# Turning the normalized tokens of a token-shift layer: TensorE transposes against DMA moves and 32x32 block transposes on VectorE

## The chip, the cores and the metric

The kernel runs on one core of one Trainium2 chip. The metric is the device time of one execution in microseconds. The core has five engines that run side by side, each with its own queue of instructions in a fixed order: TensorE (PE, its weight loads are shown as PEld), VectorE (DVE), ScalarE (ACT), GpSimd (POOL) and SyncE (SP), which here issues the DMAs. Engines wait for each other through semaphores.

## The reference

All inputs are float32. A residual stream `x` of 8 batches x 512 tokens x 512 channels goes through four blocks, each on the layer norm of the stream and scaled by the tanh of a gate: a cross attention, a routed feed-forward, a second (masked, biased) cross attention, and a token-shift feed-forward, which is the block the change is in:

```python
def _layernorm(x, axis=-1, eps=1e-05): ...      # no scale, no shift

def _L1_ffn_ref(x, W_r, W_k, W_v, mu_r, mu_k):
    x_prev = concatenate([zeros((B, 1, C)), x[:, :-1, :]], axis=1)
    xr = mu_r * x + (1.0 - mu_r) * x_prev
    xk = mu_k * x + (1.0 - mu_k) * x_prev
    r = sigmoid(einsum('btc,dc->btd', xr, W_r))
    k = einsum('btc,dc->btd', xk, W_k)
    k_act = square(relu(k))
    return r * einsum('btc,dc->btd', k_act, W_v)

x = x + tanh(g_xattn[0]) * _L0_xattn_ref(_layernorm(x), ctx_1024, ...)
x = x + tanh(g_ffn[0])   * _L0_ffn_ref(_layernorm(x), ...)
x = x + tanh(g_xattn[1]) * _L1_xattn_ref(_layernorm(x), ctx_1024, mask, ...)
x = x + tanh(g_ffn[1])   * _L1_ffn_ref(_layernorm(x), W_r, W_k, W_v, mu_r, mu_k)
```

Per batch the token-shift block is three products of 512x512 by 512x512. `mu_r` and `mu_k` are vectors over the channels.

## The kernel before, in words

The whole residual `x` stays on the chip as 32 tiles of 128 tokens x 512 channels (tokens on the partitions), four tiles a batch. The matmuls contract over the partitions, so the normalized tokens must be turned: channels on the partitions, tokens along the row. `ChannelMix` does the token-shift block. Its parts:

- `start` loads mu and the weights `wk` and `wr` on SP's queue. It runs early in the second attention, long before the block. A weight tile has 128 partitions x 4 groups x 512; channel `128 j + p` is partition p of group j.
- `normalize(t)` is one ACT instruction: `(x - mean) * rstd` of tile t, into `xn` (batch 0) or into half of a pair `xn2` (the other batches). The pairs take the buffers `v0` and `v1`, one each.
- `transpose(t)` turns a tile: four PE transposes of 128x128 against the identity into a PSUM bank (L1515) and one ACT copy of 128x512 (L1516) into `yT`, which holds the batch as 128 channels x 4 groups x (1 + 512) tokens, with a zero column in front as the previous token of the first.
- `mix_chunk(b, m, c)` forms `xk` (m = 1) or `xr` (m = 0) for a group of channels: ACT scales the shifted tokens by `1 - mu` (L1529), DVE adds the tokens times `mu` (L1532).
- `sum_steps`, `left_steps` and `right_steps` (L91, L110) form the sums of quarters that the products need, on DVE in this stage (tiles `xks`, `xrs`, and `wvs` for the sums of the squared keys).
- `SevenProducts` multiplies two 512x512 matrices with seven products of 256x256 instead of eight (a Strassen-Winograd scheme). A piece is four matmul calls of the program, eight PE instructions, into one PSUM bank. `next()` emits one piece with its evacuation. The order is 1, 2, 6, 5, 7, 4, 3: p1 and p5 are copied out by ACT (L177, L192), the others are added by DVE (L183 p2, L188 p6, L198 p7, L212 p4, L217 p3). After p7, POOL adds the copy of p5 to two quarters (L203, L204), and p4 and p3 need these sums. When a quarter is complete, `finish` applies what follows: Relu and Square on ACT for the keys (L1583, L1584), the sigmoid on ACT for the gates (L1594), and for the values DVE's multiplication by gate and `r` (L1607), POOL's addition to `x` (L1610) and the output DMA (L1619; for the last batch DVE does the addition and the DMA is L1615, and the order is 1, 6, 5, 7, 4, 3, 2).
- PSUM banks come in rotation from two pools, two of three from `p_mm` (4 buffers) and one of three from `p_s` (2 buffers), six in all; `bank()` gives the next, to pieces and to transposes.

The order of the work of every compute engine is written out by hand: `run` walks over the batches, and for batch b emits the products keys(b), gates(b), values(b). Between the seven pieces of a product it emits a list of other steps, one list a piece ("turns"). All engines' instructions come out in that order, each on its own queue:

- keys(b): `xr` of batch b (four `mix_chunk`) and its sums, and in the first batches one DVE statistics step (bn_stats, L52) for a later tile;
- gates(b): the four transposes of batch b + 1 after pieces 2, 3, 4 and 5, the four `wvs` sums after pieces 3 to 6, `xk` of batch b + 1 after pieces 6 and 7;
- values(b): the sums of `xk` of batch b + 1, then the four `normalize` of batch b + 2, and in the first batches one statistics step.

Batch 0 is normalized and turned earlier, among the last slots of the attention (`in_slot`, stage "route"); batch 1 is normalized in its "end" stage. SP's queue isn't in the hand-written order in this last part: its DMAs stand as the scheduler of the framework put them. DMAs of this program share eight completion semaphores in turn, so each may also wait for the one eight before it.

Of the kernel before, what the change touches and what calls it, by code (L numbers as in the profile page):

```python
# [9 lines left out]
FP = mybir.dt.float32  # L10
I32 = mybir.dt.int32
BF = mybir.dt.bfloat16
AF = mybir.ActivationFunctionType
# [4 lines left out]
P = 128  # L18
B, S, D = 8, 512, 512
# [3 lines left out]
TB = S // P  # L23
NC = D // P
# [196 lines left out]
class CrossAttention:  # L221
# [338 lines left out]
    def normalize(self, t):  # L560

        nc, cm = self.nc, self.cm
        xn = self.norm.tile([P, D], FP, name="xn")
        nc.scalar.activation(
            xn, cm.x[:, t, :], AF.Identity, bias=cm.nmr[:, t, :], scale=cm.rstd[:, t, :]
        )
        self.biasless.append(t)
        if not self.opening:
            self.add_bias(2)
        self.xn[t] = xn  # L570
# [422 lines left out]
class RoutedFfn:  # L993
# [20 lines left out]
    def start(self):  # L1014

        nc, tc, es, (wc_in, bc_in, tie_in) = self.nc, self.tc, self.es, self.ins[:3]
        keep = es.enter_context(
            tc.tile_pool(name="mo_keep", bufs=1, side="right", reuse_waits="tile")
        )
        self.permT = keep.tile([NE, NG, G], FP, name="permT")  # L1020
        self.bc = keep.tile([NE, 1], FP, name="bc")
        self.tie = keep.tile([NE, 1, G], FP, name="tie")
        self.keep = keep
        self.wc = keep.tile([P, NC, NE], FP, name="wc", tag="wc")
        self.route = es.enter_context(
            tc.tile_pool(name="mo_route", bufs=2, side="right", reuse_waits="tile")
        )
        dram = es.enter_context(
            tc.tile_pool(name="mo_x", bufs=1, space=bass.MemoryType.DRAM)
        )  # L1030
        self.aside = dram.tile([B * S, D], FP, name="aside")
        nc.sync.dma_start(out=self.wc, in_=wc_in.rearrange("(c p) e -> p c e", p=P))
        nc.sync.dma_start(out=self.bc, in_=bc_in)
        nc.sync.dma_start(out=self.tie, in_=tie_in.partition_broadcast(NE))
# [340 lines left out]
class ChannelMix:  # L1375
# [16 lines left out]
    def start(self):  # L1392
        nc = self.nc
        wr_in, wk_in, wv_in, mu_in = self.ins
        self.pool = pool = self.es.enter_context(
            self.tc.tile_pool(name="cm_w", bufs=1, side="right", reuse_waits="tile")
        )
        self.mu = pool.tile([P, 2, NC], FP, name="mu")
        nc.sync.dma_start(out=self.mu, in_=mu_in)
        self.om = pool.tile([P, 2, NC], FP, name="om")  # L1400
        self.wk = self.load(pool.tile([P, NC, D], FP, name="wk"), wk_in)
        self.wr = self.load(pool.tile([P, NC, D], FP, name="wr"), wr_in)

    def load(self, w, w_in):
        self.nc.sync.dma_start(out=w, in_=w_in.rearrange("(c p) f -> p c f", p=P))
# [86 lines left out]

    def normalize(self, t, xn=None):
        nc, cm = self.nc, self.cm
        if xn is None:
            i = t % TB
            if i % 2 == 0:
                self.two = self.at.pool.tile([P, 2, D], FP, name="xn2", tag=f"v{i // 2}")
            xn = self.two[:, i % 2, :]
        self.xn[t] = xn  # L1500
        nc.scalar.activation(
            xn, cm.x[:, t, :], AF.Identity, bias=cm.nmr[:, t, :], scale=cm.rstd[:, t, :]
        )

    def transpose(self, t):

        nc = self.nc
        b, i = divmod(t, TB)
        if i == 0:
            self.yT[b] = self.at.work.tile([P, NC, S + 1], FP, name="yT", tag="xnT")  # L1510
            nc.gpsimd.memset(self.yT[b][:, :, 0:1], 0.0)
        xn = self.xn.pop(t)
        ps = self.bank((NC, P))
        for c in range(NC):
            nc.tensor.transpose(ps[:, c, :], xn[:, c * P : (c + 1) * P], self.cm.ident)  # L1515
        nc.scalar.copy(self.yT[b][:, :, i * P + 1 : (i + 1) * P + 1], ps)  # L1516
# [309 lines left out]
```

## Time and profile before

| what | value |
|---|---|
| median of 3 runs | 1355.15 us (1353.41 to 1357.96) |
| profiled execution | 1363.44 us, span 1361.6 us |
| clock granted to TensorE | 0.991 of full speed over the span |
| ACT copies of the turned tiles (L1516) | 32 x 0.589 us |
| PE transposes of the tiles (L1515) | 128, first at 964.1 us, last at 1301.6 us |
| normalizations (L1501) | 32, median 0.81 us |
| DMAs on SP from 1062 us on | 18 outputs, median 2.8 us (512 KB) and 2.2 us (256 KB) to landing |

The page shows per engine its busy time, share of the span and number of instructions. Below that come the span in 40 equal slices, with the busy share of each in tenths (9 is 90% or more). The chain that ended last is followed back from the last instruction, at each step to what released it or to the instruction ahead of it on its engine. Groups of instructions are listed as line, engine, operation, output<-input, shape and count, then busy us and mean ns of one, then the idle time before them and what ended it. A busy PE is not PE at its peak, since the ends of matmuls are modelled. The view by stretches gives for each stretch its length, then for PE, PEld, DVE, ACT and POOL the busy us with the number of instructions, then the granted clock, the share of DMA and GB/s. In a timeline a line is start, length, engine, line and what it does, and in square brackets how long the engine was idle before and what ended that.

### The profile page before, as it was taken

What the parts mean: (1) busy time and instruction counts of PE and PEld (TensorE: products, weight loads), DVE (VectorE), ACT (ScalarE), POOL (GpSimd) and SP (SyncE); (2) the same over time, 40 slices, a digit from 0 to 9 for tenths busy, and PEclk for the clock granted to TensorE, in tenths of its full rate; (3) what the DMA queues carried; (4) which work ended last, traced back from release to release, by engine and by line L of the source; (5) the groups of instructions that cost most, each with busy time, mean ns of one, the idle gap of its engine ahead of it and who ended that gap; (6) DMA issues with size and microseconds to landing.
All of it is one profiled execution on the core that took longest, in us unless ns stands there. A gap on an engine that the chain in (4) does not pass through costs nothing. (4 is left out here: it accounts for less than half of the span.)

```text
span 1361.6 us, 32823 instructions
## 1 busy us (share of the span) xinstructions
PE 1300.3 (95%) x13184; PEld 1031.4 (76%) x13184; DVE 1001.3 (74%) x1448; ACT 808.0 (59%) x2538; POOL 702.0 (52%) x624
## 2 busy tenths in 40 slices
PE   6998899999999988999999999999999999999997
PEld 6886677777776877888888666676766888888886
DVE  4876667777786676777788777777775787887776
ACT  1365878888774435444225778888875454554442
POOL 4854555655643001555797777777665234443331
PEclk9999999999999999999999989999999999999999
DMA  9501566666612356431401067667610000000000
GB/s 295 200 1 40 192 203 226 210 209 202 207 55 64 110 160 218 125 115 63 153 1 63 29 193 225 213 215 224 215 44 1 1 32 31 32 32 32 31 32 32
DMA packets 116237, 160.84 MB, mean 118 GB/s; under 512 B 6973, under 2 KB 71997, under 8 KB 116085
## 3 DMA queue, kind: packets, MB, share of 16 engines
q1 hardware_dynamic: 115797, 158.74, 36.0%
q8 instruction: 104, 1.70, 0.5%
q14 instruction: 48, 0.39, 0.1%
q10 hardware_dynamic: 288, 0.00, 0.0%
HBM read 93.84 MB, written 64.88 MB: 117 GB/s over the span
## 5 line engine op out<-in xcount | busy, mean ns | idle before, releaser
L721 ACT ACTIVATE pr<-s,nmx 128x120 f32<-128x120 f32 x768 | 273.0, 496 | 41.8 <-DVE nmx L710 26.3
L878 PE MATMUL ops<-wo,aT 128*128 128x512 f32 x512 | 240.3, 611 | 5.7 <-DVE prT L842 2.8
L731 POOL TENSOR_TENSOR pr<-pr,rs 128x960 f32<-128x960 f32 x88 | 160.0, 1820 | 141.6 <-DVE rs L727 139.8
L721 ACT ACTIVATION_READ_ACCUMULATOR pr<-s,nmx 128x1 f32 x768 | 194.1, 253 | 0.0
L878 PEld LDWEIGHTS ops<-wo,aT 128*128 128x128 f32 x512 | 93.3, 192 | 104.2 <-issue 91.1
L1349 POOL TENSOR_TENSOR r<-r,b 128x1024 f32<-128x1024 f32 x31 | 73.5, 2377 | 148.5 <-ACT r L1348 148.5
L710 DVE TENSOR_REDUCE nmx<-s 128x8 f32<-128x960 f32 x96 | 106.6, 1153 | 55.1 <-PE s L666 55.0
L793 DVE STREAM_TRANSPOSE pr<-pr 128x1024 f32<-128x1024 f32 x88 | 109.1, 1240 | 33.1 <-POOL pr L731 33.1
L165 PE MATMUL qps<-xnT,wq 128*128 128x256 f32 x512 | 119.0, 380 | 0.0
L165 PEld LDWEIGHTS qps<-xnT,wq 128*128 128x128 f32 x512 | 96.3, 189 | 23.3 <-issue 10.0
L52 DVE BATCH_NORM_STATS2 bnst<-x 128x6 f32<-128x512 f32 x128 | 87.5, 684 | 0.3
L759 POOL TENSOR_TENSOR pr<-pr,rs 128x960 f32<-128x960 f32 x32 | 58.1, 1822 | 41.0 <-DVE rs L758 30.7
L861 PE MATMUL aps<-prT,v 120*32 120x128 f32 x2048 | 70.1, 278 | 9.1 <-DMA prT<-plane 4.1
L1610 POOL TENSOR_TENSOR x<-x,cv 128x512 f32<-128x512 f32 x28 | 41.4, 1480 | 70.8 <-DVE cv L1607 70.8
L888 DVE SCALAR_TENSOR_TENSOR x<-ops,gates,x 128x512 f32<-128x512 f32 x64 | 47.9, 748 | 38.8 <-PE ops L878 38.3
L666 PE MATMUL s<-kT,qT 32*128 32x120 f32 x2048 | 73.9, 280 | 0.3 <-ACT pr L721 0.3
L666 PEld LDWEIGHTS s<-kT,qT 32*128 32x128 f32 x2048 | 67.4, 190 | 7.2 <-issue 5.3
L861 PEld LDWEIGHTS aps<-prT,v 120*32 120x32 f32 x2048 | 52.7, 110 | 22.7 <-issue 11.2
L1348 ACT COPY r<-rps 128x1024 f32<-128x1024 f32 x31 | 31.4, 1013 | 59.1 <-PE rps L1336 59.1
L1583 ACT ACTIVATE kT<-kT 128x512 f32<-128x512 f32 x32 | 20.1, 627 | 73.5 <-DVE kT L183 38.4
L1336 PE MATMUL rps<-ident,rT 128*128 128x128 f32 x512 | 61.9, 275 | 1.8 <-DVE rT L1316 1.4
L769 ACT ACTIVATE pr<-s,nmx 128x120 f32<-128x120 f32 x128 | 44.2, 371 | 29.0 <-DVE nmx L766 29.0
(239 smaller groups left out, 3139.9 us busy)
## 6 DMA issues: line engine op xcount, KB each, us to landing
plane<-pr SPq DMA_DIRECT2D x88, 512.0 KB, 3.5
prT<-plane SPq DMA_DIRECT2D x176, 240.0 KB, 4.0
w<-in_w_dram SPq DMA_DIRECT2D x32, 512.0 KB, 4.6
x<-in_x_dram SPq DMA_DIRECT2D x8, 1024.0 KB, 16.9
aside<-x SPq DMA_DIRECT2D x32, 256.0 KB, 3.1
x<-aside SPq DMA_DIRECT2D x8, 1024.0 KB, 10.2
out_dram<-x SPq DMA_DIRECT2D x14, 512.0 KB, 2.8
wk<-in_wk_dram SPq DMA_DIRECT2D x3, 1024.0 KB, 8.6
```

The source lines that it names most:

```text
L52: cm.nc.vector.bn_stats(st, cm.x[:, t, :])
L165: self.nc.tensor.matmul(ps[:, m, :], rows[:, k, m * n : (m + 1) * n], columns[:, k, :], start=(k == 0), stop=(k == 1),)
L666: nc.tensor.matmul(s[j // 2][:, j % 2, hc * LK : (hc + 1) * LK], self.qT[b][r : r + 32, hc, toks], self.kT[r : r + 32, hc, keys], start=no ...
L710: nc.vector.tensor_reduce(nmx[u], sv[u], AX.X, ALU.max, negate=True)
L721: nc.scalar.activation(dst, src, AF.Exp, bias=nmx[u][:, j, hc, :], accum_out=sm[:, u, j, hc : hc + 1],)
L731: nc.gpsimd.tensor_tensor(half[u], half[u], by, ALU.mult)
L759: nc.gpsimd.tensor_tensor(pr[:, js, :, :], pr[:, js, :, :], rs[:, js, :, :].to_broadcast([P, 2, NC, LK]), ALU.mult,)
L793: nc.vector.transpose(pr, pr)
L861: nc.tensor.matmul(out, self.v[b // 2][:LK, b % 2, h * HD : (h + 1) * HD], p, start=True, stop=True,)
L878: nc.tensor.matmul(ops, self.aT[t][:, c, :], self.wo[:, c, :], start=(c == 0), stop=(c == NC - 1),)
L1336: nc.tensor.transpose(ps[:, k // 4, (k % 4) * P : (k % 4 + 1) * P], self.rT[:, 16 * tq + 8 * h + k, :], self.cm.ident,)
L1349: nc.gpsimd.tensor_tensor(r, r, b2, ALU.add)
```

## The change

Tiles of batches 1 to 7 are no longer turned by PE. A transposition of 128x128 is split into two steps: a move that brings blocks of 32 tokens to the right quarter of the partitions, and a transposition within 32x32 blocks.

- `normalize` is as before, but after each second tile `move_rows` follows: SP writes the pair (256 tokens x 512 channels) to a DRAM tile `rows` and reads it back with four DMAs, one for each quarter q of 32 partitions, into a new tile of the same buffer. Partition `32 q + e` then holds, for the eight groups of 32 tokens, token e of the group and the 128 channels `128 q` to `128 q + 127` (512 bytes each).
- `transpose` for b > 0 is one DVE instruction of 128x512 (sixteen 32x32 blocks for each quarter) that writes straight into `yT`. The PSUM bank, the four PE transposes and the ACT copy are gone. It stands at the same places in the program's order.
- Channels lie differently now: group j of partition `32 q + e` is channel `128 q + 32 j + e`. So `wk` and `wr` are loaded with four DMAs each (`load_rows`), mu with eight, and batch 0, which PE still turns, is written by `normalize` in an order of channels that gives the same places.

In the built program PE has 112 transposes fewer, ACT 28 copies fewer and DVE 28 transposes more; the order of the others on PE, DVE, ACT and POOL is unchanged. In the gates DVE's order becomes L183, transpose, L188, wvs, transpose, wvs, transpose, L198, wvs, transpose, L212. On SP, from the second moved batch on, the order is: write of the first pair, write of the second, four reads of the first, two output DMAs, four reads of the second.

```diff
@@ class ChannelMix, start
-        nc.sync.dma_start(out=self.mu, in_=mu_in)
+        for m in range(2):
+            by_row = mu_in[:, m, :].rearrange("(j e) q -> q e j", j=NC)
+            for q in range(4):
+                nc.sync.dma_start(out=self.mu[32 * q : 32 * q + 32, m, :], in_=by_row[q])
         self.om = pool.tile([P, 2, NC], FP, name="om")
-        self.wk = self.load(pool.tile([P, NC, D], FP, name="wk"), wk_in)
-        self.wr = self.load(pool.tile([P, NC, D], FP, name="wr"), wr_in)
+        self.wk = self.load_rows(pool.tile([P, NC, D], FP, name="wk"), wk_in)
+        self.wr = self.load_rows(pool.tile([P, NC, D], FP, name="wr"), wr_in)
+
+    def load_rows(self, w, w_in):
+        rows = w_in.rearrange("(q j e) f -> q e j f", q=4, j=NC)
+        for q in range(4):
+            self.nc.sync.dma_start(out=w[32 * q : 32 * q + 32], in_=rows[q])
+        return w
@@ normalize
-        if xn is None:
-            i = t % TB
+        moved = xn is None
+        i = t % TB
+        if moved:
             if i % 2 == 0:
                 self.two = self.at.pool.tile([P, 2, D], FP, name="xn2", tag=f"v{i // 2}")
             xn = self.two[:, i % 2, :]
         self.xn[t] = xn
+        to, x = xn, cm.x[:, t, :]
+        if not moved:
+            to = xn.rearrange("p (j q e) -> p q j e", q=4, j=NC)
+            x = x.rearrange("p (q j e) -> p q j e", q=4, j=NC)
         nc.scalar.activation(
-            xn, cm.x[:, t, :], AF.Identity, bias=cm.nmr[:, t, :], scale=cm.rstd[:, t, :]
+            to, x, AF.Identity, bias=cm.nmr[:, t, :], scale=cm.rstd[:, t, :]
         )
+        if moved and i % 2:
+            self.move_rows(t - 1)
+
+    def move_rows(self, t):
+        nc = self.nc
+        plane = self.at.dram.tile([2 * P, D], FP, name="rows")
+        nc.sync.dma_start(out=plane.rearrange("(i p) d -> p i d", p=P), in_=self.two)
+        two = self.at.pool.tile([P, 2, D], FP, name="xn2", tag=f"v{t % TB // 2}")
+        quarters = plane.rearrange("(i e) (q d) -> q e i d", e=32, q=4)
+        for q in range(4):
+            nc.sync.dma_start(
+                out=two[32 * q : 32 * q + 32].rearrange("p i (q d) -> p (i q) d", q=4),
+                in_=quarters[q],
+            )
+        for n in range(2):
+            self.xn[t + n] = two[:, n, :]
@@ transpose
         xn = self.xn.pop(t)
+        if b > 0:
+            to = self.yT[b][:, :, i * P + 1 : (i + 1) * P + 1]
+            nc.vector.transpose(
+                to.rearrange("p j (q t) -> p q j t", q=4),
+                xn.rearrange("p (q j e) -> p q j e", q=4, j=NC),
+            )
+            return
         ps = self.bank((NC, P))
```

## The prediction

> **What bounds the kernel now.** I read the page first, then the chain that ended last, then one batch of the last stage engine by engine, then the waits. The page's engine line and its slices of TensorE say that PE is full almost everywhere, the last stage included:
>
> ```profile
> PE 1300.3 (95%) x13184; PEld 1031.4 (76%) x13184; DVE 1001.3 (74%) x1448; ACT 808.0 (59%) x2538; POOL 702.0 (52%) x624
> PE   6998899999999988999999999999999999999997
> ```
>
> The change works in the token-shift layer, from about 1040 us on. There a batch is three products of seven pieces (keys, gates, values), and the four transposes of the next batch stand among the pieces of the gates. I cut the stage at each start of the DVE instruction of L198 in the gates (piece p7); the view by stretches gives (span, then busy us of PE, PEld, DVE, ACT, POOL):
>
> ```profile
> 1185.36:1224.11 38.75, 38.57 (x186) 33.46 (x185) 31.46 (x44) 20.15 (x36) 16.04 (x15) 1.00 0.07 28
> 1224.11:1262.87 38.76, 38.57 (x186) 33.45 (x185) 29.91 (x40) 20.16 (x36) 14.11 (x11) 1.00 0.08 28
> 1262.87:1301.62 38.75, 38.58 (x186) 33.47 (x185) 29.88 (x41) 20.16 (x36) 14.09 (x11) 1.00 0.07 27
> 1301.62:1340.18 38.56, 38.56 (x182) 33.99 (x181) 29.74 (x40) 16.36 (x29) 14.05 (x10) 1.00 0.08 28
> ```
>
> Two things are to be seen. The first row has 1.55 us more DVE work (bn_stats) than the second, and the span is the same: DVE instructions that fall into its waits cost nothing. And the last row, which leads into batch 7, holds no transposes on PE and no yT copies on ACT (ACT 16.36 instead of 20.16); it is 0.2 us shorter, no more. So a loop that needs no PE transposes already takes 38.56 us. The chain names it; a batch's part of it:
>
> ```profile
> 1182.59 0.70 DVE r L183
> 1183.38 0.69 DVE r L188
> 1184.70 0.69 DVE wvs L91
> 1185.40 0.67 DVE r L198
> 1186.20 1.59 POOL r L203
> 1187.81 0.70 DVE r L212
> ```
>
> From 1070 us to 1299 us the chain holds DVE, ACT and POOL and no PE. The loop is: ACT's Relu and Square of the last keys, ACT's copy L177, DVE L183, L188, two wvs sums, L198, POOL L203, ACT sigmoid and xk scaling, DVE through the values and the next keys, back to ACT. The same stretch of DVE for the gates of batch 7, by the timeline:
>
> ```profile
> 1337.46 0.69 DVE L183 TENSOR_TENSOR r<-r,cps 128x512 f32<-128x512 f32 x1 [1.23 <-ACT r L177]
> 1338.25 0.69 DVE L188 TENSOR_TENSOR r<-r,cps 128x512 f32<-128x512 f32 x1
> 1338.86 0.69 DVE L91 TENSOR_TENSOR wvs<-kT 128x512 f32<-128x512 f32 x1
> 1339.58 0.69 DVE L91 TENSOR_TENSOR wvs<-wvs,kT 128x512 f32<-128x512 f32 x1
> 1340.18 0.68 DVE L198 TENSOR_TENSOR r<-r,cps 128x512 f32<-128x512 f32 x1
> 1340.78 0.68 DVE L91 TENSOR_TENSOR wvs<-kT 128x512 f32<-128x512 f32 x1
> 1342.63 0.69 DVE L212 TENSOR_TENSOR r<-r,cps 128x512 f32<-128x512 f32 x1 [1.16 <-POOL r L203]
> ```
>
> From L183 to L198 DVE has no gap; after L198 it waits 1.16 us for POOL. PE, though full, waits on this loop for its PSUM banks (PEld waits over six batches):
>
> ```profile
> PEld cps L165 <- DVE kT L217: 2.1, 6, 0.4
> PEld cps L165 <- DVE r L183: 1.8, 6, 0.3
> PEld cps L1515 <- ACT r L177: 1.2, 6, 0.2
> ```
>
> That is 5.1/6 = 0.85 us of a batch, all in the gates, where the transposes take banks too.
>
> **The change, part by part.** *Removed from PE:* 112 transposes, seven batches of 16. Sixteen take 38.57 - 36.2 = 2.4 us of PE with their waits, where 36.2 is 168 matmuls at 46.64/216 = 0.216 us (the chain's unbroken end). All but 0.2 us of that is hidden by the DVE loop: gain 38.76 - 38.56 = 0.2 us a batch. *Removed from ACT:* 28 copies of 0.589 us; the next ACT instruction on the loop, the sigmoid L1594, waits 1.4 us for POOL L203 after them, so nothing.
>
> *Added to DVE:* 28 block transposes of 128x512. The nearest row is the same instruction at twice the size (first line; below it the PE form that goes):
>
> ```profile
> L793 DVE STREAM_TRANSPOSE pr<-pr 128x1024 f32<-128x1024 f32 x88 | 109.1, 1240 | 33.1 <-POOL pr L731 33.1
> L1515 PE MATMUL cps<-ident,xn 128*128 128x128 f32 x112 | 17.0, 274 | 0.0
> ```
>
> Half of 1.24 us is 0.62; with the same fixed part as the 0.69 us sums of 512 elements, which leaves 0.70. Neighbours that don't depend on each other start 0.08 us before the end of the one ahead (0.69 long, 0.61 apart), so a transpose takes 0.54 to 0.62 us of the queue. I take 0.62, the end with a fixed part. In the order of the built kernel they stand T1 after L183, T2 between the two wvs sums, T3 before L198, T4 after the third wvs. L183 to L198 takes 0.79 + 0.61 + 0.72 + 0.60 = 2.72 us now. The 0.79 and 0.72 hold the wait for the instruction just ahead, which T1 and T2 fill. After it is four instructions at 0.60 and three at 0.62: 4.26 us, so +1.54. T4 falls into the 1.16 us wait for POOL and costs nothing while it is under that. T1 and T3 wait for four DMAs each; three extra semaphore instructions of 21 ns (as the profile shows on L793) before each make up to 0.13 us. I take +1.54 + 0.12 - 0.2 = **+1.46 us a batch**, ends 1.1 (0.54 each, waits free) and 2.1 (0.70 each, dependent spacing).
>
> *Where it counts.* Gates of batch 0 (1062 to 1070 us) are bound by PE: DVE waits 1.41 us before L188 and 2.31 before L198. Three transposes fewer ahead of p7, at 0.44 us each (four start 0.44 us before the next matmul), are -1.3 us, and T1 to T3 fit in 3.7 us of waits. The gates of batches 1 to 6 each pay: 6 x 1.46 = +8.8. Gates of batch 7 have no transposes. At the end DVE waits 1.84 us for PE before L198 of the last values; a late DVE uses that up, since PE, rid of its transposes, is ahead by then: -1.8. The rest of the end is DVE without gaps. Sum: -1.3 + 8.8 - 1.8 = **+5.7 us**.
>
> *DMA.* Each batch gains 2 writes and 8 reads on SP's queue; SP has only two output DMAs a batch there. Issue by rows: 0.37 us for a write, 0.36 to 0.84 for a read. Landing: 3.5 us for 512 KB (plane), 3.5 to 5.6 for 240 KB (prT), 7.8 to 12.7 for 1 MB in 512-byte pieces (x from aside). In the batch at 1185, normalized tiles are ready at 1198.2 and 1199.6. The first pair is read by about 1205 + 5.6 = 1210.6 (at worst 1218); L183 runs at 1221.3. The second pair's reads stand on SP behind the two output DMAs, which wait for POOL L1610 until 1208.9: issued by 1213.0, landed by 1218.6, at worst 1225.7; T3 would run at 1225.0. So 6.4 us to spare, at worst 0.7 late: zero. Nothing urgent is queued behind on SP; the next writes are 30 us away. Batch 1's pairs are normalized by 1046.0; eight reads, 6.7 us of issue and 5.6 of landing give about 1063, T3 runs at 1066.
>
> *Weights and mu:* 3 DMAs become 16 on SP between 698.6 and 716 us; the next on that queue is at 776.8, and 13 more at 0.84 are 11 us. Zero. The permuted writes of four normalizations (0.81 us on ACT) are taken as before.
>
> *A rule against the change.* PE's 16 transposes and DVE's four cost alike (2.4 and 2.5 us), but PE's were covered. The Trainium skill, "VectorE: DVE Perf Modes", section "Rules for kernel authors", says to use TensorE for a 128x128 transpose where PSUM will do. Its section "The three transpose paths" prices 128x128 in bf16 at 311 ns on VectorE and 390 on TensorE; by it twelve blocks on the loop would be an estimated 3.7 us a batch, and the sum +19 us. The f32 row above gives 1.24 us for eight blocks, 0.155 each, so I keep the row.
>
> **The rivals.**
> 1. *PE is the bound (faster).* For it: 38.57 us busy of 38.76. If the loop shrinks once PE runs ahead, a batch falls to 36.2: 7 x 2.5 = -17, 1338 us. It decides if DVE's handoff waits (6.9 us a batch) hang on PE; the stretch without transposes (38.56) speaks against it.
> 2. *The DVE transposes are hidden.* 6.9 us of waits would hold four; then only -1.3 - 6 x 0.2 = -2.5, 1352.7. Against it: T1 to T3 stand where DVE has no gap.
> 3. *The transpose is slower in this shape.* Its output goes in runs of 32 elements to four planes, which L793 doesn't do. At 1.24 us each: 3 x 0.62 x 6 = +11.2 more, 1372.
> 4. *The moved rows arrive late.* From a landing of 12 us on, each us late is 6 us in all; at 2 us late 1373.
>
> **How the numbers follow.** The profiled execution took 1363.44 us (span 1361.6), 8.3 above the median of the runs, 1355.15; I add the difference to the median: 1355.15 + 5.7 = **1360.8**. With the batch cost from 1.1 to 2.1 and the gain of batch 0 in doubt: +3.5 to +11, 1358.6 to 1366. Forecast 0.58, rival 1 0.15, rival 2 and what lies between 0.12, rivals 3 and 4 0.15. The range 1353 to 1371 leaves out rival 1 and the far part of 3 and 4. The measurement tells 0.3%, 4.1 us, from no change: slower by more (over 1359.2) is most of the forecast and rivals 3 and 4, 0.68; within 0.15, mostly rival 2; faster 0.17.
>
> **What would show it.** Right: from L198 of the gates to the next 40.2 us; T1, T2, T3 back to back with their neighbours at 0.70 us, T4 inside the wait for POOL; PE with gaps of 3 to 4 us a batch; no DVE wait on a DMA. Wrong: a span of a batch under 38.5 (rival 1), transposes of 1 us and more (rival 3), a DVE wait for xn2 (rival 4).

## The result and the profile after

The changed kernel takes 1368.3 us (median of 6 runs, 1363.98 to 1370.81) against 1358.1 us for the kernel before on the same chip (6 runs): a ratio of 1.0071, 95% interval [1.0047, 1.0095]. Run again beside other kernels it gave 1.0061 [1.0045, 1.0076]. The change makes the kernel slower by 0.6 to 0.7%, the direction and mechanism that were forecast; the forecast of 1360.8 us was a median of 1355.15 us for the kernel before plus 5.7 us.

The profiled execution took 1363.98 us (span 1362.0, granted clock 0.994), hardly more than the 1363.44 us of the profiled execution before. The reason lies ahead of the change's stage: the first instruction of the stage that both have (DVE L888) starts at 1042.54 us here and at 1048.54 us there. Over the twelve traces of this study this start goes with the clock granted to the profiled execution, not with the change: 1046.5 to 1048.5 us in the seven traces at 0.991 or 0.992, 1042.1 to 1044.7 us in the five at 0.993 or 0.994. In the rows of the stage the clock is 1.00. So all comparisons of traces below run from that instruction to the end of the span: 313.06 us before, 319.46 us after, **+6.40 us**.

The page's engine line of the changed kernel shows the transfer of work, and nothing of its price:

```profile
PE 1290.1 (95%) x13072; PEld 1015.0 (75%) x13072; DVE 1016.8 (75%) x1476; ACT 792.4 (58%) x2510; POOL 702.0 (52%) x624
```

PE lost 112 instructions and 10 us, ACT 28 and 16 us, DVE gained 28 and 15.5 us. What counts is seen in the stretches from L198 of the gates to the next (span, then busy us of PE, PEld, DVE, ACT, POOL, then clock, DMA share and GB/s):

```profile
1182.23:1222.37 40.14, 37.96 (x170) 31.34 (x169) 33.62 (x49) 18.05 (x30) 16.04 (x15) 1.00 0.25 79
1222.37:1262.49 40.12, 37.94 (x170) 31.33 (x169) 32.03 (x44) 18.05 (x30) 14.09 (x11) 1.00 0.25 79
...
1302.62:1341.14 38.52, 36.28 (x163) 30.12 (x162) 30.33 (x42) 15.23 (x26) 14.04 (x10) 1.00 0.08 28
```

A batch takes 40.13 us instead of 38.75, and only the stretch into batch 7, which transposes nothing, is as long as before. The first row has 1.6 us more DVE work than the second (bn_stats) and the same span, as before: DVE still has places where work is free. The transposes are not in them, as DVE's timeline shows (start, length, engine, line, operation; in square brackets the idle time before and what ended it):

```profile
1218.14 0.69 DVE L183 TENSOR_TENSOR r<-r,cps 128x512 f32<-128x512 f32 x1 [1.23 <-ACT r L177]
1218.75 0.70 DVE L1547 STREAM_TRANSPOSE yT<-xn 128x512 f32<-128x512 f32 x1
1219.38 0.65 DVE L188 TENSOR_TENSOR r<-r,cps 128x512 f32<-128x512 f32 x1
...
1220.55 0.70 DVE L1547 STREAM_TRANSPOSE yT<-xn 128x512 f32<-128x512 f32 x1
...
1221.74 0.70 DVE L1547 STREAM_TRANSPOSE yT<-xn 128x512 f32<-128x512 f32 x1
1222.37 0.65 DVE L198 TENSOR_TENSOR r<-r,cps 128x512 f32<-128x512 f32 x1
1222.94 0.68 DVE L91 TENSOR_TENSOR wvs<-kT 128x512 f32<-128x512 f32 x1
1223.53 0.70 DVE L1547 STREAM_TRANSPOSE yT<-xn 128x512 f32<-128x512 f32 x1
1224.78 0.69 DVE L212 TENSOR_TENSOR r<-r,cps 128x512 f32<-128x512 f32 x1 [0.55 <-POOL r L203]
```

From the start of L183 to that of L198 it is 4.23 us, with seven instructions and no gap (2.72 us in the stretch that the prediction shows, which has no transposes). The fourth transpose lies in the wait for POOL, which shrinks from 1.16 to 0.55 us and delays nothing.

The moves through DRAM don't show in DVE's waits. The list of DMA issues of the changed kernel (count, size of each, median us from issue to landing) has them at:

```profile
rows<-xn SPq DMA_DIRECT2D x14, 512.0 KB, 2.8
...
xn<-rows SPq DMA_DIRECT2D x56, 128.0 KB, 3.4
```

### The profile page after: what moved, and what is told of

Its sections match the earlier page's. It is cut to its first block, busy times and chain, and to the rows that moved or that the text cites. A ratio compares the mean times of both kernels' runs of the same rounds, so it can differ in the third digit from the quotient of the medians.

```text
span 1362.0 us, 32794 instructions
## 1 busy us (share of the span) xinstructions
PE 1290.1 (95%) x13072; PEld 1015.0 (75%) x13072; DVE 1016.8 (75%) x1476; ACT 792.4 (58%) x2510; POOL 702.0 (52%) x624
## 5 line engine op out<-in xcount | busy, mean ns | idle before, releaser
L721 ACT ACTIVATE pr<-s,nmx 128x120 f32<-128x120 f32 x768 | 272.9, 496 | 40.3 <-DVE nmx L710 24.7
L793 DVE STREAM_TRANSPOSE pr<-pr 128x1024 f32<-128x1024 f32 x88 | 109.1, 1240 | 32.3 <-POOL pr L731 32.3
L165 PEld LDWEIGHTS qps<-xnT,wq 128*128 128x128 f32 x512 | 96.3, 189 | 23.3 <-issue 10.3
L888 DVE SCALAR_TENSOR_TENSOR x<-ops,gates,x 128x512 f32<-128x512 f32 x64 | 47.9, 748 | 37.3 <-PE ops L878 36.8
L1346 DVE TENSOR_TENSOR r<-rps,b 128x1024 f32<-128x1024 f32 x33 | 40.4, 1225 | 28.3 <-PE rps L1336 28.3
```

Source lines behind the costliest of these rows:

```text
L165: self.nc.tensor.matmul(ps[:, m, :], rows[:, k, m * n : (m + 1) * n], columns[:, k, :], start=(k == 0), stop=(k == 1),)
L721: nc.scalar.activation(dst, src, AF.Exp, bias=nmx[u][:, j, hc, :], accum_out=sm[:, u, j, hc : hc + 1],)
L793: nc.vector.transpose(pr, pr)
```

## The experiments

The theory: the loop DVE - ACT - POOL bounds the stage, three of the four transposes stand in it and cost what they take of DVE's queue; everything else of the change is about free. The rivals: PE is the bound or close to it; the moves, the weights' new layout or the transposes' shape cost something of their own. "Batch" below is the span from L198 of the gates to the next, and "the stage" the time from DVE L888 to the end, less the 313.06 us of before.

**The transposes at places where DVE waits.** The first transpose goes after the fifth piece of the keys, the next two after the seventh, and the fourth stays behind L198.

```diff
@@ run, keys(b)
+                if b + 1 < B:
+                    t = TB * (b + 1)
+                    turns[4].append(lambda t=t: self.transpose(t))
+                    turns[6].append(lambda t=t + 1: self.transpose(t))
+                    turns[6].append(lambda t=t + 2: self.transpose(t))
@@ run, gates(b)
-                    turns[n + 1].append(step)
+                    if b == 0:
+                        turns[n + 1].append(step)
+                    elif n == TB - 1:
+                        turns[4].append(step)
```

> The same work as the changed kernel, three of four block transposes of a batch moved from the gapless stretch of DVE in the gates (L183 to L198) into DVE's waits: one into the wait for POOL in the keys, two into the wait for ACT's copy at the end of the keys; the fourth stays in the wait for POOL in the gates. Theory (place decides): a batch from L198 of the gates to the next falls from 40.14 us to 38.6 to 38.8, six times 1.4 = 8.4 us less than the changed kernel; from the trace's +6.4 us against the kernel before this gives -2 us, a ratio of 0.9985. Rival (the moves and the added DVE work cost, wherever they stand): the ratio stays where the change put it, 1.005 to 1.0095.

Measured: 0.9988 [0.9973, 1.0004], batch 38.66 to 38.69 us, stage -2.28 us. The same 28 transposes on the same engine cost nothing there, as the next experiment, without any, confirms. Stretch and DVE timeline of this kernel, from L217 of the keys to L183 of the gates:

```profile
1218.66:1257.34 38.68, 37.06 (x170) 31.62 (x169) 32.28 (x44) 18.05 (x30) 14.11 (x11) 1.00 0.26 82
```

```profile
1213.44 0.67 DVE L217 TENSOR_TENSOR kT<-kT,cps 128x512 f32<-128x512 f32 x1
1214.03 0.68 DVE L91 TENSOR_TENSOR xrs<-xr,xrs 128x512 f32<-128x512 f32 x1
1214.64 1.29 DVE L1547 STREAM_TRANSPOSE yT<-xn 128x512 f32<-128x512 f32 x2
1215.94 0.69 DVE L183 TENSOR_TENSOR r<-r,cps 128x512 f32<-128x512 f32 x1
```

Two transposes (1.29 us together) fill the 1.23 us that DVE otherwise waits ahead of L183. With the same engine and the same work, the place decides.

**No transposes at all.** The moves stay; `yT` of the moved batches is set to zero by POOL.

```diff
-            nc.gpsimd.memset(self.yT[b][:, :, 0:1], 0.0)
+            nc.gpsimd.memset(self.yT[b] if b > 0 else self.yT[b][:, :, 0:1], 0.0)
...
-            nc.vector.transpose(
-                to.rearrange("p j (q t) -> p q j t", q=4),
-                xn.rearrange("p (q j e) -> p q j e", q=4, j=NC),
-            )
```

> No transposes for batches 1 to 7 on any engine, so yT is not computed there: it is only filled with zeros by a POOL memset. Normalizations and DMA moves stay. Theory (a DVE, ACT and POOL loop bounds the stage): a batch takes 38.5 us as the stretch without transposes did; gates of batch 0 -1.3, six batches -0.2 each, end -0.6: -3.1 us against the kernel before, ratio 0.998. Rival (PE is the bound): a batch takes 36.2 us, -17 us, ratio 0.987. If the moves themselves cost, the time lies above the kernel before.

Measured: 0.9982 [0.9967, 0.9998], batch 38.67 us, stage -2.41 us:

```profile
1220.98:1259.65 38.67, 37.06 (x170) 31.64 (x169) 29.83 (x40) 18.06 (x30) 15.80 (x11) 1.00 0.27 82
```

With the transposes gone from PE and DVE alike, and the DMAs still running, a batch is 0.08 us shorter than before. So PE's transposes were worth no more than that, and the first rival (36.2 us a batch) falls. The kernel with the hidden transposes, in which DVE does read the moved rows, has the same stage within 0.13 us. So neither the moves nor waits for them leave a cost that these traces show.

**The same work twice, at two places.** The first transpose of each batch is done twice, or the fourth.

```diff
-            nc.vector.transpose(
+            for _ in range(2 if i == 0 else 1):      # the other kernel: i == 3
+                nc.vector.transpose(
```

> The changed kernel with the first block transpose of each batch issued twice (same result), where DVE has no gap. Theory: +0.62 us a batch, 40.76 us from L198 to L198, +3.7 us over the changed kernel. Rival (only DVE's total load counts): the same time as with the fourth issued twice.

> The changed kernel with the fourth block transpose of each batch issued twice, inside DVE's wait for POOL after L198. 0.54 us of that wait are left and the second one takes 0.62: theory +0.08 us a batch, 40.22 us, +0.5 us over the changed kernel. Rival (only DVE's total load counts): +3.7 us as with the first issued twice.

Measured: with the first twice 1.0078 [1.0052, 1.0104], batch 40.87 us, stage +10.85 us; with the fourth twice 1.0058 [1.0035, 1.008], batch 40.19 to 40.22 us, stage +7.25 us. The stretches of the one and of the other:

```profile
1224.85:1265.72 40.87, 38.38 (x170) 31.18 (x169) 32.76 (x46) 18.05 (x30) 14.09 (x11) 1.00 0.25 77
```

```profile
1226.89:1267.11 40.22, 38.03 (x170) 31.35 (x169) 32.57 (x46) 18.05 (x30) 14.09 (x11) 1.00 0.26 79
```

One more transpose between L183 and L198 costs 40.87 - 40.13 = 0.74 us a batch, one more behind L198 0.08. Both have the same number of DVE instructions (x46), so it is the place that counts. The 0.74 is more than the 0.62 expected: a transpose and its repeat take 1.45 us together in both kernels, two transposes of different tiles only the 1.29 us shown above. That the repeat has to follow the first because both write the same place is likely, but not shown. The 0.08 came out as expected partly by luck: with a second one of 0.75 us, L198 to L212 grew from 2.41 to 2.54 us, and 0.05 of that was made up later in the batch. The intervals of the two ratios overlap, so it is the traces that tell the two apart, not the times.

**A shorter loop, first try.** If the loop is the bound, it should be possible to beat the kernel before. Built on the kernel with hidden transposes: the two `wvs` sums that stand between L188 and L198 move behind L198.

```diff
-            for n, step in enumerate(squares):
-                turns[n + 2].append(step)
+            for n, step in zip((4, 4, 5, 6), squares):
+                turns[n].append(step)
```

> As the kernel with the hidden transposes, and in the gates the wvs sums (left sums of the squared keys, L91) moved too: the first two from before L198 to after it, the third after L212, the fourth after L217, so that L183 to L198 of DVE is 1.5 us instead of 2.7. Theory (what stands between L183 and L198 on DVE is on the loop): a batch falls by 1.2 us from 38.67 to 37.4 or 37.5, six batches, so 7 us under the hidden version and 9 us under the kernel before, ratio 0.993 to 0.9945. Rival (PE, or ACT's chain, takes over as the bound): the batch stays above 38 us, ratio 0.998.

Measured: 0.9993 [0.9977, 1.0009], batch 38.57 us, stage -0.96 us. The expectation was missed. DVE's timeline of this kernel, and POOL's at the same time:

```profile
1216.61 0.69 DVE L198 TENSOR_TENSOR r<-r,cps 128x512 f32<-128x512 f32 x1
1217.22 0.68 DVE L91 TENSOR_TENSOR wvs<-kT 128x512 f32<-128x512 f32 x1
1217.93 1.64 DVE L91 TENSOR_TENSOR wvs<-wvs,kT 128x512 f32<-128x512 f32 x1
1219.50 0.70 DVE L1547 STREAM_TRANSPOSE yT<-xn 128x512 f32<-128x512 f32 x1
1220.13 0.64 DVE L212 TENSOR_TENSOR r<-r,cps 128x512 f32<-128x512 f32 x1
```

```profile
1217.45 1.58 POOL L203 TENSOR_TENSOR r<-r,q 128x512 f32<-128x512 f32 x1 [5.35 <-DVE r L198]
1218.99 1.72 POOL L204 TENSOR_TENSOR r<-r,q 128x512 f32<-128x512 f32 x1
```

The second `wvs` sum now starts while POOL's L203 runs. It takes 1.64 us instead of 0.69 and ends 0.54 us after L203, and POOL's L204 takes 1.72. L198 to L212 becomes 3.52 us where the kernel with hidden transposes has 2.44, which gives back nearly all that the shorter way from L183 to L198 gained (1.58 us instead of 2.72).

**The same move of the sums on the kernel before,** with PE's transposes: the same edit of `squares`.

> The kernel before, with only the wvs sums of the gates moved as in the packed version; PE still turns the tiles. Theory: the DVE loop would be 37.4 us, but PE's own work with its transposes is 36.2 + 16 x 0.11 = 38.0 us a batch, so PE becomes the bound: 38.0 to 38.5 us, ratio 0.997 to 0.999. Rival (PE's transposes are free whatever DVE does): 37.4 us as in the packed version, ratio 0.993 to 0.9945.

Measured: 1.0024 [1.0011, 1.0037], batch 39.15 us, stage +2.42 us. It has the same collision of DVE and POOL, and besides DVE waits 1.3 us for PE ahead of L198. Two effects at once, so it does not answer whether PE's transposes hold back a shorter loop.

**The new layout of weights and mu alone.** The weights and mu are loaded as in the changed kernel and every normalization is written in the permuted order, but nothing is moved and PE turns all batches.

```diff
-        moved = xn is None
+        moved = False
+        pair = xn is None
...
-        if b > 0:
+        if False:
             to = self.yT[b][:, :, i * P + 1 : (i + 1) * P + 1]
```

> The kernel before with the new places of the channels alone: wk and wr by four DMAs each, mu by eight, and every normalization (all 32, not only four) written in the permuted order; PE turns all tiles, no moves, no block transposes. Theory: no difference from the kernel before, ratio 0.998 to 1.002, a batch of 38.76 us. Rival (part of the measured 10 us, beyond the 6.4 us of the trace, lies in the loads or the permuted writes): up to +4 us, ratio 1.003.

Measured: 1.0015 [1.0, 1.003], batch 38.73 us, stage +0.09 us. In the stage the layout is free; the permuted normalizations take 0.804 us (median), those of the kernel before 0.81. The ratio's interval touches 1. These runs were granted a lower clock than those of the kernel before beside them (mean 0.9919 against 0.9936); at equal clock, by the line worked out under "The absolute time" below, nothing is left of the difference (0.0 us, give or take 0.9).

**The changed kernel once more,** beside these experiments.

> The changed kernel again, beside the others on the same chip. Theory (the trace's difference from the first common instruction of the stage to the end is the whole cost): +6.4 us, ratio 1.0047. Rival (a further cost outside the stage): +10 us, ratio 1.007; then the time up to the L888 instruction at about 1045 us is later than in the kernel before.

Measured for the changed kernel beside these: 1.0061 [1.0045, 1.0076], batch 40.13 us, stage 319.39 - 313.06 = +6.33 us. The rival's sign is not there: L888 starts at 1047.01 us, not later than the 1048.54 us of the kernel before.

**A shorter loop, second try.** Only one `wvs` sum and the last two transposes stand beside POOL's L203, and the second sum comes behind L212. Against the kernel with hidden transposes:

```diff
@@ run, keys(b)
-                    turns[6].append(lambda t=t + 2: self.transpose(t))
@@ run, gates(b)
-            for n, step in enumerate(squares):
-                turns[n + 2].append(step)
+            for n, step in zip((4, 5, 6, 6), squares):
+                turns[n].append(step)
...
-                    elif n == TB - 1:
+                    elif n >= TB - 2:
```

> Block transposes and wvs sums placed anew: beside POOL's L203 in the gates stand only the first wvs sum and two block transposes (one input each, 0.70 us beside POOL in every trace so far); the second wvs sum, which took 1.64 us beside POOL in the packed version, goes behind L212, the third and fourth behind L217; one block transpose each stays in the keys' wait for POOL and in the wait for ACT's copy. L183 to L198 has nothing but L188 between. Theory (what cost the packed version its gain was the two-input sum beside POOL): a batch of 37.5 us against 38.67 with the transposes hidden, six times 1.17: 7 us less, and with the hidden version's -2 us a ratio of 0.9925 to 0.9945 to the kernel before. Rival (another wait of the loop, PE's pieces or ACT's chain, closes in): 38 us and more, ratio 0.997 to 0.999.

Measured: **0.994 [0.9922, 0.9959]**, 1351.6 us against 1358.75; batch 37.56 us, stage -7.56 us. This version beats both kernels. Its stretch, its DVE timeline, and one line of its chain of work:

```profile
1213.37:1250.94 37.57, 36.94 (x170) 31.68 (x169) 32.26 (x44) 18.16 (x31) 14.12 (x11) 1.00 0.27 84
```

```profile
1212.58 0.69 DVE L188 TENSOR_TENSOR r<-r,cps 128x512 f32<-128x512 f32 x1
1213.37 0.69 DVE L198 TENSOR_TENSOR r<-r,cps 128x512 f32<-128x512 f32 x1
1213.97 0.69 DVE L91 TENSOR_TENSOR wvs<-kT 128x512 f32<-128x512 f32 x1
1214.58 1.30 DVE L1547 STREAM_TRANSPOSE yT<-xn 128x512 f32<-128x512 f32 x2
1215.83 0.69 DVE L212 TENSOR_TENSOR r<-r,cps 128x512 f32<-128x512 f32 x1
```

```profile
1206.49 21.00 PE cps L165 x96
```

L198 follows L188 directly, the two transposes take 1.30 us beside L203 of POOL (1214.20 to 1215.79 us), and L212 starts as soon as POOL is done. L183 to L198 is 1.58 us, where the kernel with hidden transposes has 2.72, and the rest of the loop, from L198 to the next L183, takes 36.0 us in both: the whole gain lies in the part that was shortened.

The line of the chain seems to say that PE bounds the loop now, with twelve pieces without a break up to L198 of the values. The timelines of PE and of DVE say otherwise:

```profile
1206.49 5.45 PE L165 MATMUL cps<-wrs,xrs 128*128 128x256 f32 x24 [0.36 <-DVE xrs L91]
...
1222.13 1.89 PE L165 MATMUL cps<-wvs 128*128 128x256 f32 x8
```

```profile
1226.40 1.17 DVE L110 TENSOR_TENSOR xks<-xks,xk 128x512 f32<-128x512 f32 x1
1227.49 0.68 DVE L198 TENSOR_TENSOR cv<-cv,cps 128x512 f32<-128x512 f32 x1
```

The twelve begin with p6, p5 and p7 of the gates, so they are the last five of the gates and all seven of the values. The piece that this L198 adds (p7 of the values, the second row) had ended at 1224.02 us, and DVE comes to L198 straight from a sum of its own. PE in turn waits for DVE's second sum of `xr` in each batch. So the loop of DVE, ACT and POOL still bounds this version, at 37.56 us; PE's own work (busy 36.94 us) is close behind.

**Whether that needs the transposes off PE.** The same places of the `wvs` sums on the kernel before.

```diff
-            for n, step in enumerate(squares):
-                turns[n + 2].append(step)
+            for n, step in zip((4, 5, 6, 6), squares):
+                turns[n].append(step)
```

> The kernel before, PE transposes included, with the wvs sums of the gates placed as in the version with two block transposes beside POOL. Theory (PE is the next bound behind the DVE loop): the loop would allow 37.4 us, PE needs 36.2 + 16 x 0.11 = 38.0 us and its waits for banks: 38.0 to 38.5 us a batch, ratio 0.997 to 0.999. Rival (PE's transposes stay free): 37.5 us, ratio 0.9945 or less.

Measured: 0.9998 [0.9982, 1.0014], batch 38.74 us, stage +0.05 us. Neither expectation held: the shorter way of DVE gives nothing at all here. Its stretch, and its chain at the gates:

```profile
1183.26:1222.01 38.75, 38.57 (x186) 33.45 (x185) 31.41 (x43) 20.12 (x36) 16.05 (x15) 1.00 0.07 28
```

```profile
1218.73 0.48 ACT r L177
1219.24 0.70 DVE r L183
1219.93 0.04 issue
1219.98 2.01 PE cps L165 x8
```

DVE's L198 of these gates, and below it L183 and L198 of the gates of batch 6 in the kernel before:

```profile
1222.01 0.69 DVE L198 TENSOR_TENSOR r<-r,cps 128x512 f32<-128x512 f32 x1 [1.29 <-PE cps L165]
```

```profile
1298.84 0.69 DVE L183 TENSOR_TENSOR r<-r,cps 128x512 f32<-128x512 f32 x1 [1.24 <-ACT r L177]
...
1301.62 0.69 DVE L198 TENSOR_TENSOR r<-r,cps 128x512 f32<-128x512 f32 x1
```

PE enters the loop between L183 and L198: the weight loads of one piece wait 0.30 us for DVE's L183, the piece takes 2.01 us, and L198 waits 1.3 us for it. By the code this is p7, whose PSUM bank is the one that L183 frees when the transposes take banks in the rotation too; that the bank is the cause is argued from the code, the wait itself is measured. By way of PE, then, L183 to L198 takes 2.77 to 2.78 us, here and in the other kernel with the sums moved and the transposes on PE, though DVE is ready 1.3 us earlier. In the kernel before it takes the same 2.77 to 2.78 us in batches 1 to 6, and 2.72, DVE's own four instructions, wherever PE has no transposes (batch 7, and the kernels with hidden or without transposes). So in the kernel before PE and the DVE loop were all but level at 38.7 us. The transposes' way off PE is worth 0.08 us a batch while the loop is 38.7 us, and 38.74 - 37.56 = 1.18 us once the loop is shorter. A kernel that leaves the transposes on PE and gives them PSUM banks outside the rotation of the pieces was not run, so it is not shown that they must leave PE for this gain.

## Why the prediction was right, and where it was off

The prediction's sum against the trace, by its own steps:

| step | predicted us | measured us, before to after |
|---|---|---|
| gates of batch 0 | -1.3 | 20.55 to 19.24: -1.31 |
| six batches | 6 x 1.46 = +8.8 | 232.53 to 240.84: +8.31, 1.385 each |
| stretch into batch 7 | 0 | 38.56 to 38.52: -0.04 |
| the end | -1.8 | 21.42 to 20.86: -0.56 |
| sum | +5.7 | +6.40 |

*What bounds the stage.* Right: the chain of the kernel before held DVE, ACT and POOL, and with no transposes a batch stays at 38.67 us. PE's busy share of 99.5% did not decide it. What the prediction did not see is that PE was a second bound at nearly the same length: it held L198 of the gates 2.78 us behind L183, where DVE alone needed 2.72. Only the kernels with the sums moved and the transposes still on PE showed this. And the removal of PE's transposes gained 0.08 us a batch, not the 0.2 of the sum: the stretch into batch 7, from which the 0.2 was read, is also 0.14 us shorter from L198 to the next L183 (35.84 us against 35.98), with PE's transposes and without.

*The price of a transpose.* Taken as 0.70 us long and 0.62 us of the queue, from half of the 1240 ns of the 128x1024 form. The group in the changed kernel's profile (busy us, mean ns):

```profile
L1547 DVE STREAM_TRANSPOSE yT<-xn 128x512 f32<-128x512 f32 x28 | 19.7, 702 | 0.0
```

They start 0.62 to 0.63 us before what follows. L183 to L198 is 1.51 us longer than in the stretch without transposes, where 1.54 was reckoned, and 1.45 us longer than in the batches that it replaces. The third rival, a slower transpose because of the four output planes, falls. The Trainium skill, "VectorE: DVE Perf Modes", section "The three transpose paths", has 311 ns for 128x128 in bf16, by which the sum would have been +19 us; a 128x128 share of the f32 row measured 702/4 = 176 ns.

*The extra waits for DMAs.* The 0.12 us a batch for them did not appear. The profile has 28 such semaphore instructions of 21 to 50 ns; the first is at 1056.7 us, while L183 (1056.67 to 1057.36 us) still runs, and the transposes start 0.61 us after L183, like any neighbour. That 0.12 was too much and the gain of 0.2 for PE's removed work was too much as well; the two errors cancel in good part, which brings 1.46 close to the 1.385 measured.

*The end, the step that failed.* The prediction let DVE's lateness vanish in its 1.84 us wait for PE before L198 of the last values, "since PE, rid of its transposes, is ahead by then". The chain of the changed kernel at that place:

```profile
1332.38 0.69 DVE xrs L91
1333.08 0.04 issue
1333.12 15.82 PE cps L165 x72
1348.94 0.02 issue
1348.97 0.70 DVE cv L198
```

PE cannot run ahead: its pieces of the last gates wait for DVE's second sum of `xr`, and from there nine pieces (15.82 us) lead straight to that L198. A late DVE makes PE late too, and of the wait only 1.84 - 1.18 = 0.66 us was used up. The term was mis-sized by 1.2 us. In the sum the six batches, reckoned 0.5 us too high, make up for some of it, so +5.7 is nearer to +6.40 than its terms are.

*The moves.* Right: 512 KB written in 2.8 us and 128 KB read in 3.4 us, no wait of DVE for them, and no cost in the kernel that keeps the moves and drops the transposes. The fourth rival falls.

*PE's gaps.* 3 to 4 us a batch were expected, 40.13 - 37.95 = 2.2 us are seen. PE's busy time fell by 0.6 us a batch only, though 2.4 us of transposes went; the ends of matmuls are modelled in the profile, and what fills the rest stays open. (The 36.2 us of the prediction should read 36.3: 168 times 0.216.)

*The rule of the skill.* "VectorE: DVE Perf Modes", section "Rules for kernel authors", prefers TensorE for a 128x128 transpose. For the change as it was made the runs agree (1.0061 and 1.0071). They no longer do when the transposes stand in DVE's waits: 0.9988 with the rest unchanged, no different from the kernel before, and 0.994 with the loop shortened.

*The absolute time.* 1368.3 us lies 7.5 us above the forecast. 3.0 us of this is the median of the kernel before, which rose from 1355.15 to 1358.1 us with more runs, and 0.7 us the sum above. The interval of the ratio, 1.0047 to 1.0095, is 6.4 to 12.9 us, with the trace's +6.40 at its lower edge, and that of the repetition, 1.0045 to 1.0076, is 6.1 to 10.3 us. What is left, 3.8 us, goes at least in part with the granted clock and not with a cost outside the stage. Beside the repetition, the 28 runs of the kernel before reach from 1363.15 us at a clock of 0.990 to 1353.4 us at 0.996, and the changed kernel had a lower clock (mean 0.9927 against 0.9936). A straight line through all these runs, with the same slope for both kernels (1.1 us for 0.001 of clock), leaves +6.6 us between them, give or take 1.0, where the stage gives +6.33. For each of the ten experiments the same estimate lies within 1 us of the difference of the stage. The first six runs of the changed kernel had a still lower clock (mean 0.9915) and lie 1.6 us above the six of the repetition, of which the line gives 1.2 us; the clocks of the kernel before beside them are not on record, so that part stays open.

## What to carry to other kernels

Price an added instruction by where it stands in its engine's order: three block transposes cost 40.13 - 38.67 = 1.46 us a batch between two links of the loop and nothing in its waits, so look for the waits of the bounding loop before choosing the engine. An engine that shows 99% busy need not be worth relieving (2.4 us of PE's work gone gave 0.08 us a batch), and one that is relieved for nothing today may be what lets the next change work: the two edits (sums out of the loop, transposes off PE) gave at most 0.1 us a batch singly and 1.2 us together. A line of the chain is a hint at what released an instruction: check against the timeline of the engine that it names. Before a late engine is allowed to "use up" a wait for another, follow what that other one waits for.

## What the runs showed of the hardware

A DVE sum of two operands that both lie in SBUF, started while a POOL sum ran, took 1.64 us instead of 0.69, and POOL's next one took 1.72 us instead of 1.27; the block transposes, with one input, took 0.65 to 0.70 us each beside the same POOL instruction. The Trainium skill states this rule ("SBUF — State Buffer", section "Who interferes with whom": a DVE instruction with two SBUF inputs contends with a GpSimd instruction that reads SBUF, one with at most one SBUF input, outside the 2-port modes, does not); the runs agree in both halves, and in this kernel it decided which work could fill a wait for POOL.
